# Four scan directions in a Mamba-like layer: two projections put into one product, and step sizes made chunk by chunk

## The chip, the cores and the metric

The kernel runs on one core of one Trainium2 chip, as one program. The metric is device time in microseconds, from three runs of the kernel before: 10589.44 us in the median, 10588.25 to 10604.14. A profile of one further execution shows where the time goes. The engines are named as in the profile: PE (TensorE, matrix products), PEld (its weight loads), DVE (VectorE), ACT (ScalarE), POOL (GpSimd) and SP (which here issues DMAs). Each engine takes its instructions in the order in which the program has them, and waits at an instruction until what it needs is there.

## What is computed

Four images of 96 channels and 64 x 64 pixels pass through six layers. The change lies in the first: a selective scan in four directions. Cut to what matters:

```python
xn = layernorm(x); xq, z = split(xn @ in_proj_w.T); z = silu(z)
xc = silu(depthwise_conv3x3(xq) + conv_b)          # 192 channels, L = 4096 pixels
x0 = xc by rows;  x1 = xc by columns
xs = [x0, x1, flip(x0), flip(x1)]                  # directions k = 0, 1, 2, 3
x_dbl = einsum('bkdl,kcd->bkcl', xs, x_proj_w)     # 6 + 16 + 16 rows per direction
dts, Bs, Cs = split(x_dbl, [6, 16, 16])
delta = softplus(einsum('bkrl,kdr->bkdl', dts, dt_w) + dt_b)   # the step sizes
h = exp(delta * A) * h + delta * u * B             # along the 4096 positions
y = sum over the 16 states of h * C, plus D * u
out = (layernorm(y0 + y1 + y2 + y3) * z) @ out_proj_w.T
```

Behind it come a deformable 3 x 3 convolution (offsets from a convolution, then gathers of pixels), a Fourier block of 192 channels, a feed-forward block, a linear attention and another feed-forward block.

## The kernel before

**Streams.** One loop (`Layer0.scan`) sets the order of everything. It goes through 1536 units: image, direction in the order 1, 3, 0, 2, four stretches of 1024 positions (backwards for directions 2 and 3), three groups of 64 channels, eight units of 8 channels x 16 states. Each unit is a load of `da` from HBM on ACT's queue (five buffers, four units ahead), an exponential on ACT (L725), a product on PE that spreads `du` (L730), on DVE a product with B (L741) and the scan (L744), on POOL a product with C (L755) and, for two units at a time, products on PE that sum the states (L772).

Between units the loop lets two other streams go on, each a chain of Python generators. `ends` prepares layer 0 for images 0, 1, 2, 3 one after another (`before`), then does the last layers of image after image, each as soon as that image is sampled. `middle` does layer 0's output part (`behind`, once the scans of the image have come far enough) and layer 1, the deformable convolution. A step of a stream is taken when the stream has credit (2.6 and 1.9 steps a unit) and while every engine has room by the costs that the steps name. A unit can be fetched only when its inputs are `ready`: while they aren't, the loop takes steps of `ends` alone, and no scan enters the order.

**The part that the change touches.** `before(b)` makes u for one image (`inputs`: normalisation and convolution; `us` holds 128 channels by rows, the same by columns, and the other 64 channels twice, by rows in the lower and by columns in the upper 64 partitions). Then it goes through 8 chunks of 512 positions twice: forwards for the pair of directions 0 and 1 (`pr` 0), backwards for 2 and 3 (`pr` 1). Directions k and k + 2 use the same u in the same order, since flipping is done by the scan, so a direction k + 2 differs from k only in its weights.

- `projected` makes, for each of the two directions of a pair, a product of 39 rows (32 of B and C, 6 of dts, one that stays 0) from two matmuls (L568 and L569, 128 and 64 channels), and ACT evicts it with a bias that makes the last row 1 (L570), into `xd0` or `xd1`, of which there is one buffer each. The 32 rows go to HBM (`bcd`).
- `steps` makes a step chain for 128 rows: t = 0 is the first direction's 128 channels, t = 1 the second's, t = 2 the other 64 channels of both. A matmul with 7 rows (L592), then on ACT abs, exp, log and two additions (L596 to L601), on DVE `rl` from `pd` and `lw` (L604), on POOL a difference (L605), on DVE another (L607: the step size, stored as `de`), on POOL the product with u (L610 or L616), and a split into three bf16 parts `du` over ACT, POOL, ACT and DVE (L622 to L628), stored on SP.
- `pipe` runs these chains four at a time, one started every three rounds. A round is one step of the stream. The order of chains in an image is one projection and three step chains, sixteen times.
- A unit of pair `pr` is ready when the two chunks under it are done up to t = 2.

After the last scan what is left is the end of image 3's output part, its layer 1, the rest of image 2's last layers and all of image 3's.

Of the kernel before, what the change touches and what calls it, by code (L numbers as in the profile page):

```python
# [8 lines left out]
F32 = mybir.dt.float32  # L9
# [24 lines left out]
NX = 2 * NS + R + 1  # L34
# [8 lines left out]
def prepare(x, **w):  # L43
# [25 lines left out]

    vecs[NX - 1, V_X1] = 1.0  # L70

# [6 lines left out]
    xp = np.concatenate([xp[:, R:], xp[:, :R], np.zeros((KG, 1, DI), f)], axis=1).transpose(0, 2, 1)  # L78
    a["xp_a"] = c(xp[:, :128].transpose(1, 0, 2))
    a["xp_c"] = c(np.stack([np.concatenate([xp[2 * p, 128:], xp[2 * p + 1, 128:]]) for p in range(2)], axis=1))  # L80
# [78 lines left out]
def cost(pe=0.0, dve=0.0, act=0.0, pool=0.0):  # L159
    return pe, dve, act, pool  # L160
# [212 lines left out]
class Layer0:  # L373
# [45 lines left out]
    def before(self, b):  # L419
        net = self.net  # L420
        tc, nc, ins = net.tc, net.nc, net.ins
        with tc.tile_pool(name=f"l0u{b}", bufs=1) as up:
# [3 lines left out]
            with tc.tile_pool(name=f"l0b{b}", bufs=1) as sm:  # L426
                xp_a, xp_c = (net.load(q, sm) for q in ("xp_a", "xp_c"))
                dtw = sm.tile([NX, KG, DI], F32, name=f"dtw{b}", tag="dtw", bufs=1)
                nc.sync.dma_start(dtw[2 * NS :], ins["dtw"])
                yield from pause(2)  # L430
                order = [(0, j) for j in range(NCH)] + [(1, j) for j in reversed(range(NCH))]
                xdbl = {}

                def chains():
                    yield self.projected(b, *order[0], us, xp_a, xp_c, sm, xdbl)
                    for n, (pr, j) in enumerate(order):
                        for t in range(3):
                            yield self.steps(b, pr, j, t, us, dtw, sm, xdbl)
                        if n + 1 < len(order):
                            yield self.projected(b, *order[n + 1], us, xp_a, xp_c, sm, xdbl)  # L440
# [115 lines left out]
    def projected(self, b, pr, j, us, xp_a, xp_c, sm, xdbl):  # L556
# [5 lines left out]
        for q in range(2):  # L562
            k = 2 * pr + q
            xd = sm.tile([NX, CH], F32, name=f"xd{b}_{k}_{j}", tag=f"xd{q}")
            hp = slice(64 * q, 64 * q + 64)
            ua = us[0][:, cs] if q == 0 else us[1][:, j * NR : (j + 1) * NR, :]
            px = net.mm(f"px{b}_{k}_{j}", NX)
            nc.tensor.matmul(px, lhsT=xp_a[:, k, :], rhs=ua, start=True, stop=False)  # L568
            nc.tensor.matmul(px, lhsT=xp_c[hp, pr, :], rhs=us[2][hp, cs], start=False, stop=True)  # L569
            nc.scalar.activation(xd, px, AF.Identity, bias=net.vec(V_X1, NX))  # L570
            xdbl[pr, j, q] = xd
            yield cost(pe=1.7, act=0.7)
        for q in range(2):
            nc.sync.dma_start(self.bc_d[b][2 * pr + q][:, cs], xdbl[pr, j, q][: 2 * NS])
        yield NOTHING

    def steps(self, b, pr, j, t, us, dtw, sm, xdbl):
# [55 lines left out]
        if t == 2:  # L633
            self.ready.add((b, pr, j))
# [895 lines left out]
```

## Time and profile before

| | us |
|---|---|
| median of three runs | 10589.44 |
| the profiled execution | 10462.69 |
| its span, first to last instruction | 10460.6 |
| DVE busy | 7640.0 (73%) |
| PE busy | 7119.7 (68%) |
| POOL busy | 6456.3 (62%) |
| ACT busy | 4352.7 (42%) |
| scans L744, 1152 + 384 | 2703.5 + 878.0 |
| projection products L568, L569, 256 records each | 234.5 + 186.3 busy |
| step products L592, 512 records | 324.5 busy |
| first scan starts at | 322.87 |
| last scan starts at | 8996 |
| last layers of image 3 alone, from about | 9790 |

A matmul with fp32 operands has two records in the trace. Busy time is the union of an engine's records, and PE's records overlap. In the profile a stretch of time is called by microseconds from the span's start. An instruction's idle time is the time in which its engine had nothing to do just before it, with the engine or DMA that ended this wait.

### The profile page before, as it was taken

The numbers are of one execution on the slowest core, as the hardware profiler recorded it, in microseconds if no ns is written. First come the engines' busy times: TensorE is split into PE (matmuls) and PEld (weight loads), VectorE is DVE, ScalarE is ACT, GpSimd is POOL, SyncE is SP. The second block draws the span as 40 slices with busy tenths as digits, with TensorE's granted clock in tenths as the row PEclk, the third lists the DMA queues.
The fourth block names the chain that finished last, engine by engine and source line by source line (L and its number), as shares of the span: only waits on it lengthen the run. The fifth ranks groups of instructions, "written<-read, shape, count | busy, mean of one in ns | idle before, by whom it ended". The sixth has DMA issues, their size and how long they took to land. (4 is left out here: it accounts for less than half of the span.)

```text
span 10460.6 us, 85850 instructions
## 1 busy us (share of the span) xinstructions
PE 7119.7 (68%) x28728; PEld 2481.0 (24%) x28728; DVE 7640.0 (73%) x4993; ACT 4352.7 (42%) x6950; POOL 6456.3 (62%) x3603
## 2 busy tenths in 40 slices
PE   7565865976794555558876665678676646877686
PEld 2010200311120111113332221133322112453262
DVE  0788688587759999987878889788888897444211
ACT  4564655665454443223433433333343423313223
POOL 0675476377537888875557878655678885366301
PEclk9555855866696666667777766677677666886695
DMA  1666565566656677776677667776767676543110
GB/s 45 166 174 157 149 173 162 140 172 168 156 134 171 184 188 185 189 181 161 177 184 184 169 160 190 172 179 166 186 174 176 174 188 151 118 137 92 52 45 6
DMA packets 775576, 1605.19 MB, mean 153 GB/s; under 512 B 249305, under 2 KB 339477, under 8 KB 773022
## 3 DMA queue, kind: packets, MB, share of 16 engines
q10 hardware_dynamic: 300672, 985.79, 37.4%
q1 hardware_dynamic: 400734, 387.34, 13.8%
q0 software_dynamic: 73728, 226.57, 8.3%
q8 instruction: 228, 3.74, 0.2%
q14 instruction: 214, 1.75, 0.1%
HBM read 1343.08 MB, written 256.29 MB: 153 GB/s over the span
## 5 line engine op out<-in xcount | busy, mean ns | idle before, releaser
L755 POOL TENSOR_TENSOR hc<-hh,bc 128x1024 f32<-128x1024 f32 x1536 | 3885.8, 2531 | 1937.3 <-DVE hh L744 1003.6
L725 ACT ACTIVATE da<-da,w_al 128x1024 f32<-128x1024 f32 x1536 | 1762.6, 1149 | 3126.4 <-DMA da<-de 981.5
L730 PE MATMUL db<-du,rep 96*128 96x512 bf16 x3072 | 1293.0, 515 | 2324.6 <-DVE hh L744 2147.1
L744 DVE TENSOR_TENSOR_SCAN hh<-da,st,db 128x1024 f32<-128x1024 f32 x1152 | 2703.5, 2347 | 165.4 <-ACT st L751 28.3
L741 DVE TENSOR_TENSOR db<-db,bc 128x1024 f32<-128x1024 f32 x1536 | 1871.0, 1218 | 585.3 <-PE db L730 585.0
L1074 POOL DMA_INDIRECT g<-table,idx x1152 | 1449.7, 1258 | 417.2 <-issue 191.1
L772 PE MATMUL py<-hc,w_fold 128*32 128x512 f32 x6144 | 1303.4, 886 | 25.4 <-POOL hc L755 8.8
L730 PEld LDWEIGHTS <-rep 96*128 96x128 bf16 x3072 | 231.2, 108 | 3539.8 <-DVE hh L744 2935.0
L744 DVE TENSOR_TENSOR_SCAN hh<-da,db 128x1024 f32<-128x1024 f32 x384 | 878.0, 2286 | 104.9 <-ACT st L751 31.5
L1085 DVE TENSOR_TENSOR g<-g,wt 128x3456 f32<-128x3456 f32 x128 | 593.1, 4634 | 148.6 <-DMA g<-table,idx 147.3
L605 POOL TENSOR_TENSOR w<-w,ex 128x512 f32<-128x512 f32 x192 | 259.0, 1349 | 650.7 <-ACT w L601 648.9
L518 PE MATMUL pc<-pad,wc 96*128 96x512 f32 x1152 | 533.1, 615 | 9.1 <-DMA wc<-wc_d 6.1
L607 DVE TENSOR_TENSOR rl<-rl,w 128x512 f32<-128x512 f32 x192 | 304.9, 1588 | 95.6 <-POOL w L605 95.3
L1102 PE MATMUL ps<-w_ident,s 128*96 128x128 f32 x1152 | 265.3, 378 | 136.9 <-DVE s L1091 120.7
L1332 POOL CAST xqf<-fl 96x512 fp8e5<-96x512 f32 x64 | 51.5, 810 | 496.6 <-DVE fl L1291 496.5
L604 DVE SCALAR_TENSOR_TENSOR rl<-pd,lw 128x512 f32<-128x512 f32 x192 | 130.7, 681 | 309.6 <-ACT lw L599 309.5
L592 PE MATMUL pd<-xd,dtw 7*128 7x512 f32 (+1 forms) x512 | 324.5, 953 | 43.9 <-ACT xd L570 28.5
L1103 ACT COPY st<-ps 96x384 f32<-96x384 f32 x384 | 177.5, 474 | 419.7 <-PE ps L1102 418.2
L772 PEld LDWEIGHTS py<-hc,w_fold 128*32 128x32 f32 x6144 | 184.8, 134 | 666.0 <-issue 516.2
L1109 PE MATMUL pd<-st,wdc 96*96 96x256 f32 x1152 | 309.0, 414 | 0.0
L518 PEld LDWEIGHTS pc<-pad,wc 96*128 96x128 f32 x1152 | 220.5, 195 | 310.5 <-issue 290.4
L628 DVE TENSOR_TENSOR du<-ex,du 128x512 bf16<-128x512 f32 x192 | 234.6, 1222 | 79.7 <-ACT du L626 75.3
(241 smaller groups left out, 10039.6 us busy)
## 6 DMA issues: line engine op xcount, KB each, us to landing
da<-de ACTq DMA_DIRECT2D x1536, 512.0 KB
du<-du ACTq DMA_DIRECT2D x384, 192.0 KB
bc<-bcd ACTq DMA_DIRECT2D x128, 512.0 KB
du<-du SPq DMA_DIRECT2D x128, 384.0 KB
y<-yb SPq DMA_DIRECT2D x384, 128.0 KB
de<-rl SPq DMA_DIRECT2D x128, 256.0 KB
m<-in_dft SPq DMA_DIRECT2D x128, 256.0 KB
du<-du SPq DMA_DIRECT2D x128, 192.0 KB
```

Source lines behind the costliest of these rows:

```text
L518: nc.tensor.matmul(pp, lhsT=wc[:, q, g * 128 : (g + 1) * 128], rhs=pad[:, r0 + dy : r0 + dy + NR, dx : dx + W], start=(q == 0), stop=(q == 8),
L592: nc.tensor.matmul(o, lhsT=dtw[2 * NS :, 2 * pr + q, m], rhs=xdbl[pr, j, q][2 * NS :], start=True, stop=True)
L607: nc.vector.tensor_sub(rl, rl, w1)
L725: self.net.nc.scalar.activation(u.da, u.da, AF.Exp, scale=self.al[:, a : a + 1])
L730: self.net.nc.tensor.matmul(db[:, h, :], lhsT=self.rep[:96, u.s % 4, :], rhs=u.du[u.s // 4][:, h * CH : (h + 1) * CH], start=True, stop=True,)
L741: nc.vector.tensor_mul(u.db, u.db, u.bc[:, 0, :])
L744: nc.vector.tensor_tensor_scan(u.along(u.hh), u.along(u.da), u.along(u.db), first, ALU.mult, ALU.add)
L755: self.net.nc.gpsimd.tensor_mul(u.hc, u.hh, u.bc[:, 1, :])
L772: nc.tensor.matmul(py[p0 : p0 + 32], lhsT=self.fold[:, u.i, :], rhs=hc[:, h * CH : (h + 1) * CH], start=u.add is None and u.i == 0, stop=( ...
L1074: nc.gpsimd.indirect_dma_start(out=g[:, k, :], out_offset=None, in_=self.tables[b % 2], in_offset=bass.IndirectOffsetOnAxis(ap=idx[:, 9 * ...
L1085: nc.vector.tensor_mul(g4, g4, w4.unsqueeze(2).to_broadcast([128, 36, C]))
L1109: nc.tensor.matmul(po, lhsT=wdc[:, k, :], rhs=st[:, k, :], start=(k == 0), stop=(k == 8))
```

## The change

The rows of directions k and k + 2 are made by one product: 32 rows of B and C and 6 of dts of direction q, the constant row at 38, zeros up to row 64, then 6 of dts of direction q + 2, a constant row at 70, and its 32 of B and C, 103 in all. The step weights of the second of the two are put at partitions 64 to 70, so that weights and rows stand in the same partitions. The loop over chunks is gone through once, forwards. A chunk has one call of `projected`, of two products (columns first), and six step chains: direction 1, the 64 other channels of 0 and 1, direction 3, the 64 of 2 and 3, direction 0, direction 2. Readiness is kept for each direction and each half of the channels (128 and 64), and a unit needs both halves of its two chunks. The cost named for a projection step goes from 1.7 to 1.9 on PE.

```diff
-NX = 2 * NS + R + 1
+NX = 64 + R + 1 + 2 * NS
...
-    vecs[NX - 1, V_X1] = 1.0
+    vecs[2 * NS + R, V_X1] = 1.0
+    vecs[64 + R, V_X1] = 1.0
...
+    xpp = np.zeros((2, NX, DI), f)
+    xpp[:, : 2 * NS] = xp[:2, R:]
+    xpp[:, 2 * NS : 2 * NS + R] = xp[:2, :R]
+    xpp[:, 64 : 64 + R] = xp[2:, :R]
+    xpp[:, 64 + R + 1 :] = xp[2:, R:]
...
-                dtw = sm.tile([NX, KG, DI], F32, name=f"dtw{b}", tag="dtw", bufs=1)
-                nc.sync.dma_start(dtw[2 * NS :], ins["dtw"])
+                dtw = sm.tile([64 + R + 1, 2, DI], F32, name=f"dtw{b}", tag="dtw", bufs=1)
+                for q in range(2):
+                    p0 = (2 * NS, 64)[q]
+                    nc.sync.dma_start(dtw[p0 : p0 + R + 1], ins["dtw"][:, 2 * q : 2 * q + 2])
...
-                order = [(0, j) for j in range(NCH)] + [(1, j) for j in reversed(range(NCH))]
...
-                    yield self.projected(b, *order[0], us, xp_a, xp_c, sm, xdbl)
-                    for n, (pr, j) in enumerate(order):
-                        for t in range(3):
-                            yield self.steps(b, pr, j, t, us, dtw, sm, xdbl)
-                        if n + 1 < len(order):
-                            yield self.projected(b, *order[n + 1], us, xp_a, xp_c, sm, xdbl)
+                    yield self.projected(b, 0, us, xp_a, xp_c, sm, xdbl)
+                    for j in range(NCH):
+                        for ks in ((1,), (0, 1), (3,), (2, 3), (0,), (2,)):
+                            yield self.steps(b, ks, j, us, dtw, sm, xdbl)
+                        if j + 1 < NCH:
+                            yield self.projected(b, j + 1, us, xp_a, xp_c, sm, xdbl)
...
-        for q in range(2):
-            k = 2 * pr + q
-            xd = sm.tile([NX, CH], F32, name=f"xd{b}_{k}_{j}", tag=f"xd{q}")
+        for q in (1, 0):
+            xd = sm.tile([NX, CH], F32, name=f"xd{b}_{q}_{j}", tag=f"xd{q}")
...
-            nc.tensor.matmul(px, lhsT=xp_a[:, k, :], rhs=ua, start=True, stop=False)
-            nc.tensor.matmul(px, lhsT=xp_c[hp, pr, :], rhs=us[2][hp, cs], start=False, stop=True)
+            nc.tensor.matmul(px, lhsT=xp_a[:, q, :], rhs=ua, start=True, stop=False)
+            nc.tensor.matmul(px, lhsT=xp_c[hp], rhs=us[2][hp, cs], start=False, stop=True)
...
-            yield cost(pe=1.7, act=0.7)
-        for q in range(2):
-            nc.sync.dma_start(self.bc_d[b][2 * pr + q][:, cs], xdbl[pr, j, q][: 2 * NS])
+            yield cost(pe=1.9, act=0.7)
+        for q in (1, 0):
+            nc.sync.dma_start(self.bc_d[b][q][:, cs], xdbl[q, j][: 2 * NS])
+            nc.sync.dma_start(self.bc_d[b][q + 2][:, cs], xdbl[q, j][64 + R + 1 :])
...
-            nc.tensor.matmul(
-                o, lhsT=dtw[2 * NS :, 2 * pr + q, m], rhs=xdbl[pr, j, q][2 * NS :], start=True, stop=True
-            )
+        for k in ks:
+            h, q = divmod(k, 2)
+            o, m = (pd[64 * q : 64 * q + 64], slice(128, DI)) if both else (pd, slice(0, 128))
+            rows = slice(64, 64 + R + 1) if h else slice(2 * NS, 2 * NS + R + 1)
+            nc.tensor.matmul(o, lhsT=dtw[rows, q, m], rhs=xdbl[q, j][rows], start=True, stop=True)
...
-        if t == 2:
-            self.ready.add((b, pr, j))
+        self.ready.update((b, k, both, j) for k in ks)
...
-                while not all((u.b, u.k // 2, 2 * u.j + h) in self.ready for h in range(2)):
+                while not all(
+                    (u.b, u.k, both, 2 * u.j + h) in self.ready for both in (False, True) for h in range(2)
+                ):
```

## The prediction

> **What bounds the kernel now.** I read four views in this order: the page (which engine is full, and when), the windows by stage, the waits of each stage, the timeline at the start. From the page:
>
> ```profile
> span 10460.6 us, 85850 instructions
> ...
> DVE  0788688587759999987878889788888897444211
> POOL 0675476377537888875557878655678885366301
> ...
> L604 DVE SCALAR_TENSOR_TENSOR rl<-pd,lw 128x512 f32<-128x512 f32 x192 | 130.7, 681 | 309.6 <-ACT lw L599 309.5
> L744 DVE TENSOR_TENSOR_SCAN hh<-da,st,db 128x1024 f32<-128x1024 f32 x1152 | 2703.5, 2347 | 165.4 <-ACT st L751 28.3
> ```
>
> VectorE carries the run of 1536 scans (one product at 1.22 us and one scan at 2.3 us each, about 3.55 us a unit) and is the fullest engine in most slices from the second to the 35th. Before it lies a start of 323 us, behind it a tail from 8996 us on. I cut the run at the scans between which a stage of the other work stands (columns: stretch, its length, busy us and counts of PE, weight loads, DVE, ACT, POOL, then clock, DMA share, GB/s):
>
> ```profile
> 323.00:422.00 99.00, 53.12 (x144) 7.58 (x144) 84.14 (x59) 54.14 (x88) 72.28 (x38) 0.60 0.64 173
> 1223.00:1761.00 538.00, 346.77 (x826) 52.88 (x830) 437.19 (x307) 328.61 (x523) 385.08 (x226) 0.59 0.64 171
> 1761.00:2063.00 302.00, 255.40 (x738) 82.45 (x730) 192.14 (x128) 167.54 (x197) 117.81 (x55) 0.84 0.53 141
> 2785.00:3093.00 308.00, 277.17 (x781) 88.46 (x780) 173.55 (x113) 166.16 (x220) 113.60 (x55) 0.89 0.53 135
> 3546.00:4074.00 528.00, 300.08 (x922) 67.39 (x919) 505.05 (x292) 246.60 (x397) 421.57 (x252) 0.62 0.69 184
> ```
>
> Row 1 is the first 20 units of image 0. Row 2 is the stage that the change rewrites, for image 1: 81 units in 538 us, 6.64 us each, DVE 81% busy. Row 3 is the convolution of image 2, PE at 85%, DVE waiting. Row 4 is the convolution of image 3 with the offset convolution of layer 1 on top, PE at 90%. Row 5 is image 3's steps beside sampling, DVE at 96%. So time here is DVE's work plus DVE's idle time, and only edits of that idle time count. The waits of row 2 and row 4 say what it is (us in total, times, longest):
>
> ```profile
> DVE rl L604 <- ACT lw L599: 35.3, 13, 15.8
> DVE rl L607 <- POOL w L605: 31.4, 26, 2.0
> DVE du L628 <- ACT du L626: 27.4, 10, 16.6
> ...
> PE db L730 <- DVE hh L744: 167.2, 55, 10.2
> ...
> ACT ex L596 <- PE pd L592: 27.6, 14, 4.7
> ...
> DVE db L741 <- PE db L730: 119.6, 29, 15.8
> ```
>
> In row 2 the scan's own input is early (PE waits 167 us for DVE); DVE loses its time inside the step chains, to ScalarE, which itself waits for the projections' and step products on PE. The last line is row 4: there PE is the bound.
>
> **What the Trainium skill says.** "Perfetto Trace Analysis", section Optimization Strategy: take the most contended engine, look at its gaps, and where regimes differ interleave them. The trace agrees that there are regimes (DVE 96% in row 5, 56% in row 4). "TensorE: Matmul & The Clock Gate", section LDWEIGHTS: a weight load is priced by its columns, not its rows; by it, 103 columns for 39 would add an estimated 53 ns a load. In the trace a load of 39 columns takes 141 ns (median, L568), more than the page's price, the loads of 128 and 64 columns at L592 a median of 184; both stand beside running matmuls, so I charge nothing. "GPSIMD Engine Reference", section Specifications: GpSimd shares VectorE's SBUF interface when DVE has two SBUF inputs. The trace agrees: L607 takes 0.69 us with POOL idle, 1.62 us beside it, 1588 ns on average. So packing chains denser doesn't cost DVE only its bare time; I use 3.5 us a chain (679 + 1588 + 1222 ns).
>
> **The change, part by part.**
>
> 1. Projections. Two directions in one product: 128 products fall away on PE (two records each, 0.95 us by the means 1012 and 817 ns, so 1.8 us: 235 us of PE) and 64 evictions on ACT (0.68 us: 44 us). A product over 512 columns costs the same with 103 output rows as with 39, by L592, whose 128 rows take a median of 1056 ns against 1047 for L568. Neither engine bounds these stages, so only the DVE waits behind them count. I sorted the idle time before the 192 instructions at L604 by their place among the three of a chunk: of 30, 35, 55 and 19 us for the images (the 170 us before the very first one left out) about 14, 27, 26 and 14 stand at the first, directly behind the projections; of L628's waits 8, 25, 12 and 7 at the third, whose bf16 casts share ACT with the evictions. That is some 130 us at 64 boundaries. Half the boundaries go: I take -55 us, from -20 (the chain merely waits for POOL instead) to -80.
>
> 2. Order by chunks, start. In the built program 10 chains instead of 7 stand ahead of the first scan, 22 instead of 13 ahead of scan 20, 34 instead of 19 ahead of scan 44: a unit needs both halves of its direction for two chunks, and a chunk now makes four directions first. Between the groups the scan stops in the program's order. Alone, chains run like this:
>
> ```profile
> 282.22 0.69 DVE L604 SCALAR_TENSOR_TENSOR rl<-pd,lw 128x512 f32<-128x512 f32 x1 [1.22 <-ACT lw L599]
> 285.54 0.68 DVE L604 SCALAR_TENSOR_TENSOR rl<-pd,lw 128x512 f32<-128x512 f32 x1
> 292.21 0.68 DVE L604 SCALAR_TENSOR_TENSOR rl<-pd,lw 128x512 f32<-128x512 f32 x1
> 302.34 0.69 DVE L604 SCALAR_TENSOR_TENSOR rl<-pd,lw 128x512 f32<-128x512 f32 x1 [1.22 <-ACT lw L599]
> ```
>
> Three chains in 20.1 us, 6.7 each, of which DVE works 3.5. Some 13 chains more run that way (3 ahead of the first scan, about 10 in two new pauses): 13 x 6.7 = 87 us of scan-free time, of which 13 x 3.5 = 46 us is DVE work that would have stood between scans anyway. Net +41 us, less up to 10 that units in flight cover, plus about 5 us for each restart, when ACT's queue holds the next loads behind the last step's store (at the first start a load kept ACT 18 us): +40 us. Bounds: -5, if flying units fill the pauses; +87, if the lighter units later don't run faster.
>
> 3. Order, later images. The rounds of a preparation fall from 192 to 168 (three per chain or projection: 64 against 56), so the stream gets on. Image 3's chains end at scan 512, not 603; its convolution starts about scan 345, beside layer 0's output part, and no longer beside the offset convolution (row 4, 120 us of DVE waiting for PE; row 3, the convolution without it, 79). Its chains then lie beside the offset convolution, where PE has the removed 60 us to spare. Against that, fewer chains lie in the full row 5. I count -25 us, from -60 to +30: no row shows this mixture, so rows 3 and 4 bound it.
>
> 4. Tail. Behind the last scan stand 32 fewer of the Fourier products (8 groups at about 1.1 us) and two more output products with their gating: -5 us, from -20 to 0.
>
> Nothing for the rest: as many stores of B and C rows (128), as many step stores on SP, one more weight load per image, all beside scans; if SP ran late it would show at ACT's loads, priced in 2. The unit of work per scan is unchanged.
>
> Sum: -55 + 40 - 25 - 5 = -45 us on the profiled execution's 10460.6, 0.43%. That execution took 10462.7 us in all, 1.2% below the 10589.4 median of the shown runs; I carry the ratio over: 10589.4 x 0.9957 = 10544.
>
> **Rivals.**
> Slower: the start decides. For: the pauses are in the order, and units 96 to 111, with hardly any chain beside them, still took 5.5 us. Against: units 0 to 44 ran at 4.7 with one chain to three. Price: +87, relief only -20, no gain by mixing: +67 us, 10657. It decides once lightened units stay above 5.2 us.
> No change: ACT and PE relief are swallowed, because chains come denser (image 1's 48 from scan 140 to 211 instead of 164 to 240) and L607 waits for POOL more; -20 + 40 - 15 - 5 = 0, 10590. For: POOL is at 72% in row 2 and its w-waits are already 31 us.
> Much faster: the pauses are filled and the mixture pays in full: -70 + 0 - 60 - 15 = -145, 10443. Against: the two pauses are six chains long, and only about two units fly.
> That the edit doesn't remove the products can't be: 128 instead of 256 stand on PE.
>
> **How the numbers follow.** Forecast 0.50 (its own range 10480 to 10590), slower 0.25, no change 0.17, much faster 0.08. The range 10450 to 10665 reaches the slower case and nearly the much faster one. A difference under 0.2% (21 us) can't be told from none here: faster 0.57, same 0.17, slower 0.26.
>
> **What would show it.** Projections: 128 records each at the two product lines, and DVE's waits of image 1's stage down from 94 us to about 70. Start: first scan near 338 us, DVE gaps near units 20 and 44, image 0's last chain near 790 us (831 now), its scan 96 no later than 880. Mixture: DVE waiting for PE during image 3's convolution under 120 us. I am wrong if scan 160 comes over 40 us late without being regained by scan 700, or if the time per unit in the stages of steps doesn't fall below 6.6 us.

## The result, and the profile after

The changed kernel takes 10632.65 us in the median of four runs (10618.27 to 10648.25), beside four runs of the kernel before at 10588.85 us (10575.49 to 10604.14). The ratio is 1.0041, with a 95% interval from 1.0021 to 1.0062: slower by about 44 us, where 45 us less had been forecast. Run again, on a chip where the kernel before takes about 10490 us, the changed kernel had the ratio 1.0053 (1.0034 to 1.0071). The record names no chip for the first runs. The profile of before, 10462.69 us, lies in the range of the later runs of that kernel (10458.58 to 10523.74) and not in that of its own (10575.49 to 10604.14), so it may belong to another chip than they do.

The page of the profile after; of the groups, those that answer to the lines shown of before:

```profile
span 10616.5 us, 85396 instructions
...
DVE  0787777687678999978888898787898977134211
...
POOL 0674665576467888845568888555688875156201
...
L755 DVE TENSOR_TENSOR_SCAN hh<-da,st,db 128x1024 f32<-128x1024 f32 x1152 | 2703.7, 2347 | 262.4 <-ACT st L762 91.0
...
L755 DVE TENSOR_TENSOR_SCAN hh<-da,db 128x1024 f32<-128x1024 f32 x384 | 878.1, 2287 | 53.0 <-ACT da L736 8.2
...
L614 DVE SCALAR_TENSOR_TENSOR rl<-pd,lw 128x512 f32<-128x512 f32 x192 | 131.3, 684 | 293.2 <-ACT lw L609 280.3
```

And of before, the scans that start without a state:

```profile
L744 DVE TENSOR_TENSOR_SCAN hh<-da,db 128x1024 f32<-128x1024 f32 x384 | 878.0, 2286 | 104.9 <-ACT st L751 31.5
```

Lines have moved: L604 of before is L614, L607 is L617, L628 is L638, L744 is L755. The digits of VectorE's first slices are lower (the second to the eleventh were 7886885877, now 7877776876), its idle time before the 1152 scans with a state has grown from 165 to 262 us, while before the 384 others it fell from 105 to 53 us: over all scans 315 us, where it was 270. The idle time before the first VectorE instruction of a chain has hardly moved, from 310 to 293 us, of which 170 us stand before the very first chain in both. The granted clock of PE is lower in this profile (0.689 on average, 0.702 before), but VectorE's idle time before the product with B, which PE ends, is nearly the same (592 us at L752, 585 at L741 before), so a slower PE shows little there.

The span of this profile is 156 us longer than that of before, more than the medians differ. Of these, 125 us lie behind the last scan (1589 us after it, 1464 before), and in the changed kernel's second profile that tail is 1501 us. So the two spans can't be subtracted. The tail of this profile is not used below, and only its part up to the last scan is read beside others.

Busy time of the changed kernel by stage (columns as in the prediction: stretch, length, busy us and counts of PE, weight loads, DVE, ACT, POOL, then clock, DMA share, GB/s). The first three rows are units 0 to 20, 20 to 44 and 44 to 96, the fourth is units 140 to 214 with image 1's step chains, the last units 399 to 462:

```profile
338.00:470.00 132.00, 69.47 (x161) 11.85 (x161) 108.67 (x77) 80.10 (x131) 93.44 (x56) 0.54 0.58 160
470.00:617.00 147.00, 84.01 (x192) 14.31 (x192) 115.58 (x84) 85.09 (x140) 102.78 (x61) 0.51 0.60 167
617.00:897.00 280.00, 139.24 (x369) 22.64 (x369) 245.78 (x187) 131.76 (x205) 186.10 (x107) 0.53 0.65 174
...
1168.00:1671.00 503.00, 279.78 (x694) 50.11 (x694) 402.58 (x292) 304.15 (x478) 365.70 (x218) 0.56 0.64 172
...
2868.00:3292.00 424.00, 285.76 (x713) 56.88 (x712) 339.93 (x251) 231.55 (x386) 281.71 (x169) 0.63 0.63 169
```

Before, units 0 to 20, 20 to 44 and 44 to 96 took 99, 109 and 320 us; the last two of these in the same view of the kernel before:

```profile
422.00:531.00 109.00, 67.55 (x175) 9.42 (x176) 98.88 (x66) 57.94 (x97) 79.91 (x42) 0.56 0.65 173
531.00:851.00 320.00, 211.65 (x462) 30.57 (x460) 271.80 (x193) 200.45 (x311) 241.54 (x142) 0.55 0.65 178
```

The two first stretches became 33 and 38 us longer and the third 40 us shorter: image 0's chains are moved ahead, and not all of the time they cost there comes back. What stands at the end of the first stretch is seen in the timeline of VectorE (start, duration; here the first instruction of each chain, then the scan's product):

```profile
430.96 0.69 DVE L614 SCALAR_TENSOR_TENSOR rl<-pd,lw 128x512 f32<-128x512 f32 x1
437.34 0.69 DVE L614 SCALAR_TENSOR_TENSOR rl<-pd,lw 128x512 f32<-128x512 f32 x1 [0.15 <-ACT lw L609]
447.48 0.69 DVE L614 SCALAR_TENSOR_TENSOR rl<-pd,lw 128x512 f32<-128x512 f32 x1 [1.22 <-ACT lw L609]
450.81 0.68 DVE L614 SCALAR_TENSOR_TENSOR rl<-pd,lw 128x512 f32<-128x512 f32 x1
457.44 0.69 DVE L614 SCALAR_TENSOR_TENSOR rl<-pd,lw 128x512 f32<-128x512 f32 x1 [0.15 <-ACT lw L609]
463.84 0.68 DVE L614 SCALAR_TENSOR_TENSOR rl<-pd,lw 128x512 f32<-128x512 f32 x1
...
468.08 1.22 DVE L752 TENSOR_TENSOR db<-db,bc 128x1024 f32<-128x1024 f32 x1
```

Six chains start in 33 us, 6.6 us apart on average, and no scan stands among them. This is the pause that the order contains.

The waits of VectorE while image 1's chains run (us in total, times, longest), in the changed kernel from 1155 to 1671 us:

```profile
DVE du L638 <- ACT du L636: 46.4, 16, 7.5
...
DVE rl L614 <- ACT lw L609: 35.8, 16, 14.4
...
DVE rl L617 <- POOL w L615: 17.7, 18, 2.0
```

Together 99.9 us, where the three lines of before had 94.1, and not the 70 of the prediction. The relief is not there.

### The profile page after: what moved, and what is told of

It reads as the page before. It is cut to its first block, busy times and chain, and to the rows that moved or that the text cites. A ratio compares the mean times of both kernels' runs of the same rounds, so it can differ in the third digit from the quotient of the medians.

```text
span 10616.5 us, 85396 instructions
## 1 busy us (share of the span) xinstructions
PE 7016.8 (66%) x28472; PEld 2521.1 (24%) x28472; DVE 7616.5 (72%) x4993; ACT 4313.2 (41%) x6886; POOL 6428.8 (61%) x3603
## 5 line engine op out<-in xcount | busy, mean ns | idle before, releaser
L741 PE MATMUL db<-du,rep 96*128 96x512 bf16 x3072 | 1296.8, 517 | 2494.0 <-DVE hh L755 2314.7
L755 DVE TENSOR_TENSOR_SCAN hh<-da,st,db 128x1024 f32<-128x1024 f32 x1152 | 2703.7, 2347 | 262.4 <-ACT st L762 91.0
L752 DVE TENSOR_TENSOR db<-db,bc 128x1024 f32<-128x1024 f32 x1536 | 1871.8, 1219 | 592.5 <-PE db L741 590.9
L783 PE MATMUL py<-hc,w_fold 128*32 128x512 f32 x6144 | 1274.0, 888 | 39.4 <-POOL hc L766 22.5
L741 PEld LDWEIGHTS <-rep 96*128 96x128 bf16 x3072 | 224.6, 107 | 3733.7 <-DVE hh L755 3095.0
L755 DVE TENSOR_TENSOR_SCAN hh<-da,db 128x1024 f32<-128x1024 f32 x384 | 878.1, 2287 | 53.0 <-ACT da L736 8.2
L604 PE MATMUL pd<-xd,dtw 7*64 7x512 f32 (+1 forms) x512 | 348.3, 1004 | 18.9 <-ACT xd L578 12.6
L1120 PE MATMUL pd<-st,wdc 96*96 96x256 f32 x1152 | 346.5, 451 | 3.2 <-issue 2.9
L638 DVE TENSOR_TENSOR du<-ex,du 128x512 bf16<-128x512 f32 x192 | 270.6, 1409 | 100.3 <-ACT du L636 92.7
L614 DVE SCALAR_TENSOR_TENSOR rl<-pd,lw 128x512 f32<-128x512 f32 x192 | 131.3, 684 | 293.2 <-ACT lw L609 280.3
L617 DVE TENSOR_TENSOR rl<-rl,w 128x512 f32<-128x512 f32 x192 | 238.7, 1243 | 105.9 <-POOL w L615 105.6
L986 PE MATMUL po<-pad,w_wom 96*27 96x512 f32 x576 | 293.3, 653 | 20.0 <-DVE rl L614 15.4
```

Of the source, the lines that this page charges most:

```text
L604: nc.tensor.matmul(o, lhsT=dtw[rows, q, m], rhs=xdbl[q, j][rows], start=True, stop=True)
L741: self.net.nc.tensor.matmul(db[:, h, :], lhsT=self.rep[:96, u.s % 4, :], rhs=u.du[u.s // 4][:, h * CH : (h + 1) * CH], start=True, stop=True,)
L752: nc.vector.tensor_mul(u.db, u.db, u.bc[:, 0, :])
L755: nc.vector.tensor_tensor_scan(u.along(u.hh), u.along(u.da), u.along(u.db), first, ALU.mult, ALU.add)
L783: nc.tensor.matmul(py[p0 : p0 + 32], lhsT=self.fold[:, u.i, :], rhs=hc[:, h * CH : (h + 1) * CH], start=u.add is None and u.i == 0, stop=( ...
L986: nc.tensor.matmul(po, lhsT=wom[:, k, :], rhs=pad[:, r0 + dy : r0 + dy + NR, dx : dx + W], start=(k == 0), stop=(k == 8),)
```

## The experiments

They ran on three chips, on each of which the kernel before takes 10487 to 10492 us in the median; each ratio is against runs of the kernel before on the same chip. The table gives from each profile when a scan starts, the time from the start of the last scan to the end of the span ("tail"), and the ratio.

| kernel | scan 0 | 44 | 96 | 609 | 882 | last scan | tail | ratio (95%) |
|---|---|---|---|---|---|---|---|---|
| before, profile shown at the start | 323 | 531 | 851 | 4074 | 5469 | 8996 | 1464 | |
| before, again | 323 | 534 | 851 | 4069 | 5470 | 9012 | 1477 | 1.0002 (0.9992 to 1.0012) |
| changed, profile above | 338 | 617 | 897 | 4106 | 5489 | 9028 | 1589 | 1.0041 (first runs) |
| changed, again | 338 | 615 | 897 | 4106 | 5492 | 9033 | 1501 | 1.0053 (1.0034 to 1.0071) |
| changed order, products apart | 348 | 644 | 927 | 4248 | 5619 | 9145 | 1520 | 1.0185 (1.0164 to 1.0206) |
| before, second pass without products | 324 | 531 | 848 | 4065 | 5465 | 9015 | 1479 | 0.9989 (0.9980 to 0.9999) |
| old order, rows kept in HBM | 322 | 531 | 850 | 4092 | 5498 | 9030 | 1487 | 1.0034 (1.0022 to 1.0046) |
| image 0 by pairs, others by chunks | 326 | 535 | 855 | 4056 | 5436 | 8995 | 1509 | 1.0007 (0.9998 to 1.0016) |
| image 0 by chunks, others by pairs | 340 | 617 | 897 | 4142 | 5519 | 9061 | 1501 | 1.0102 (1.0083 to 1.0121) |
| image 0 direction 1 first | 310 | 520 | 851 | 4063 | 5461 | 8998 | 1467 | 0.9987 (0.9977 to 0.9996) |
| image 0 by pairs, tail's order mended | 325 | 537 | 858 | 4074 | 5452 | 8993 | 1474 | 0.9986 (0.9974 to 0.9998) |
| before, tail's order spoilt | 322 | 529 | 847 | 4080 | 5470 | 9001 | 1525 | 1.0037 (1.0024 to 1.0050) |
| changed, tail's order mended | 338 | 616 | 899 | 4115 | 5488 | 9012 | 1501 | 1.0020 (1.0009 to 1.0030) |
| image 0 direction 1 first, tail's order mended | 309 | 515 | 843 | 4040 | 5433 | 8973 | 1476 | 0.9971 (0.9963 to 0.9978) |

How far a single profile may be trusted can be read from programs that are alike up to the last scan: three of before's order start it at 8996, 9012 and 9001, three of the changed order at 9028, 9033 and 9012, the two with image 0 by pairs at 8995 and 8993, the two with direction 1 first at 8998 and 8973. Up to scan 96 such programs agree within 8 us, at scan 609 within 23, and at scan 882 and the last one within 28. Smaller differences between single profiles show nothing, and ratios, which rest on several runs, are better evidence.

### The kernel before again

> The kernel before, unchanged, profiled a second time. Its first profile spans 10460.6 us with 1464 us after the last scan's start, while its other runs took 10575 to 10604 us. Theory 'the first profile was a lucky execution': this one spans about 10575 to 10600 us, with the difference of 115 to 140 us nearly all after the last scan (tail 1570 to 1600 us, as in the changed kernel, 1589) and the last scan still near 8996 us. Rival 'the change made the tail longer': this profile again has a tail of 1450 to 1480 us, and the changed kernel's 1589 us is its own loss.

It is the row "before, again" above: the ratio is 1.0002. The kernel's profile on this chip is 29 us longer than the one shown first (span 10489.4 against 10460.6), of which 16 us come in the last third of the scans and 13 us in the tail; its starts of scans in the table agree within 5 us up to 882. The short tail is there again, as the rival said. But the 1589 us don't belong to the changed kernel either: its own second profile, on the same chip as this one, has 1501.

### The changed order with the products apart

```diff
+            for p0, p1 in ((0, 39), (64, NX)):
-            px = net.mm(f"px{b}_{q}_{j}", NX)
-            nc.tensor.matmul(px, lhsT=xp_a[:, q, :], rhs=ua, start=True, stop=False)
-            nc.tensor.matmul(px, lhsT=xp_c[hp], rhs=us[2][hp, cs], start=False, stop=True)
-            nc.scalar.activation(xd, px, AF.Identity, bias=net.vec(V_X1, NX))
+                px = net.mm(f"px{b}_{q}_{j}_{p0}")[p0:p1]
+                nc.tensor.matmul(px, lhsT=xp_a[:, q, p0:p1], rhs=ua, start=True, stop=False)
+                nc.tensor.matmul(px, lhsT=xp_c[hp, p0:p1], rhs=us[2][hp, cs], start=False, stop=True)
+                nc.scalar.activation(xd[p0:p1], px, AF.Identity, bias=net.vecs[p0:p1, V_X1 : V_X1 + 1])
```

> The changed kernel with its order of chunks and chains, but each direction's 39 rows by a product of their own again: 128 products on PE and 64 evictions on ACT come back, at the same places in the order. Theory 'the merged product saves nothing, since neither engine bounds these stages': equal to the changed kernel within 15 us (ratio to before 1.003 to 1.006). Rival 'the merged product does save its 20 to 80 us, and the order costs more than it': 20 to 80 us slower than the changed kernel (ratio 1.006 to 1.012).

The ratio is 1.0185 against the changed kernel's 1.0053, slower than both expectations allowed, and the last scan starts 112 to 133 us later than in the three profiles of the changed order. That is more than twice the 55 us which the prediction gave for the products. The waits of image 1's stage, in this kernel from 1176 to 1741 us:

```profile
DVE du L639 <- ACT du L637: 68.0, 15, 8.9
ACT xd L579 <- PE px L578: 62.9, 28, 4.0
...
DVE rl L615 <- ACT lw L610: 46.8, 17, 21.6
```

In the changed kernel (again, same stage) these three are 47.5, 24.1 and 36.7 us. The products of a chunk now come in a burst: two in each of two rounds, and ScalarE, which evicts them, waits for PE and makes VectorE late. The step that makes them keeps its named cost on PE of 1.9 though it holds twice the work, so some of the loss may come from the loop's room being counted wrongly; this was not separated. So doubling the products in the *changed* order costs a great deal. That alone doesn't say that halving them in the *old* order saved as much, and the next two kernels ask for that.

### The old order without the second pass's products

```diff
         for q in range(2):
+            if pr == 1:
+                xdbl[pr, j, q] = xdbl[0, NCH - 1, q]
+                yield cost(pe=1.7, act=0.7)
+                continue
             k = 2 * pr + q
```

> The kernel before, in its own order, with the products and the evictions of the second pass left out (128 of 256 products, 64 evictions) and nothing in their place: the chains of directions 2 and 3 take the rows that the last chunk of directions 0 and 1 left, so these two directions are computed from the wrong rows. The steps of the stream and their costs stay. This is the relief of the change alone, without its order and without reloads. Theory 'the step chains don't wait for the projections in that order': scan 609 starts within 15 us of 4070 (before 4069 to 4074), the waits of DVE in image 1's stage stay at 80 to 100 us for lw, w and du together, ratio 0.998 to 1.001. Theory of the prediction (half the waits behind the projections go, 55 us): scan 609 at 3990 to 4050, the waits of image 1's stage near 70 us, ratio 0.993 to 0.997.

The ratio is 0.9989, about 12 us (1 to 21 us by the interval). Scan 609 starts at 4065, 4 to 8 us earlier than in the two profiles of before, less than such profiles differ; the last scan starts no earlier. Image 1's stage (1226 to 1755 us):

```profile
DVE du L632 <- ACT du L630: 35.0, 12, 16.2
DVE rl L608 <- ACT lw L603: 31.4, 12, 14.6
DVE rl L611 <- POOL w L609: 28.3, 24, 2.0
```

The sum is 94.7 us, against 94.1 with all the products. Over all four images, the idle time of the second pass alone at the two places that the prediction counted (the first `rl` of a chunk's first chain, the last `du` of its third) is 45 and 42 us in the two profiles of before, and 50 us here, where that pass has no product to wait for. The first theory, that the chains don't wait for the products where these are spread out, holds; the prediction's, with a ratio of 0.993 to 0.997, doesn't.

Another reading would be that a slower PE took back a larger gain. PE's granted clock is indeed lower here (0.690 to 0.696 in 14 runs, 0.699 to 0.704 in the 19 of the kernel before), and its other records are busy 79 to 93 us longer than in the two profiles of before. But VectorE's idle time before the product with B, which PE ends, is 587 us here and was 585 and 583, so there is no sign that this held VectorE up.

### The old order with the rows kept in HBM

```diff
+            if hs == (1,):
+                xd = sm.tile([64 + R + 1, CH], F32, name=f"xr{b}_{q}_{j}", tag=f"xr{q}")
+                nc.sync.dma_start(xd[dts], self.dts_d[b][q][:, cs])
+                xdbl[q, j] = xd
+                yield cost(pe=1.9, act=0.7)
+                continue
...
+            nc.sync.dma_start(self.dts_d[b][q][:, cs], xdbl[q, j][dts])
```

Products of 103 rows are made in the first pass; the second pass of an image loads its seven step rows back.

> The merged product alone: every instruction stands as in before, but the products of 103 rows are made in the first pass only; the seven rows of step sizes of directions 2 and 3 go to HBM and come back on SP in the second pass, where no product and no eviction is left (128 products and 64 evictions fewer). Theory 'PE time of the products is on the path, as the 118 us of the unmerged variant say': scan 609 starts 30 to 100 us before 4070, ratio 0.990 to 0.997. Rival 'in the old, spread order they cost only what DVE waits behind them, about 12 us an image at most': scan 609 0 to 30 us earlier, ratio 0.997 to 1.000. Below that: the reloads are late.

1.0034, so slower than before; scan 609 at 4092 is some 20 us late, which a single profile doesn't show for certain. As a test of the products' price it isn't clean, since the loads come late. The waits from 1226 to 1768 us:

```profile
DVE rl L633 <- ACT lw L628: 38.8, 14, 15.5
DVE du L657 <- ACT du L655: 36.5, 11, 16.9
DVE rl L636 <- POOL w L634: 32.4, 26, 2.0
PEld pd L623 <- DMA xr<-dts: 25.5, 6, 8.1
```

The three waits of VectorE are 107.7 us in all, not lower than before's 94.1, and the weight loads of the step products wait 25.5 us for the reloaded rows. It shows that this way of keeping the order doesn't pay; on the price of the products it decides nothing.

### Image 0 by pairs, the others by chunks, and the reverse

```diff
+                def pairs():
+                    order = [(0, j) for j in range(NCH)] + [(1, j) for j in reversed(range(NCH))]
+                    yield self.projected(b, 0, us, xp_a, xp_c, sm, xdbl, (0,))
+                    for n, (h, j) in enumerate(order):
+                        for ks in ((2 * h,), (2 * h + 1,), (2 * h, 2 * h + 1)):
+                            yield self.steps(b, ks, j, us, dtw, sm, xdbl)
...
-                yield from pipe(chains(), 4, every=3)
+                yield from pipe(pairs() if b == 0 else chains(), 4, every=3)
```

The second kernel has `chains() if b == 0 else pairs()`. In the pair order products of 103 rows are made in both passes, as many as before.

> The changed kernel, but image 0 is made in the order of before (directions 0 and 1 forwards, then 2 and 3 backwards, the products of 103 rows made in both passes); images 1 to 3 by chunks. Theory 'the start decides': scan 44 starts near 531 us as in before (617 in the changed kernel) and the whole time falls by 40 to 60 us, to before's (ratio 0.998 to 1.001). Rival 'the start is regained, the loss comes from the later images or the tail': scan 44 is early again, but the whole time stays within 15 us of the changed kernel (ratio 1.003 to 1.006).

> The complement: image 0 by chunks as in the changed kernel, images 1 to 3 in the order of before with products of 103 rows in both passes. Theory 'the start decides': as slow as the changed kernel (ratio 1.003 to 1.006), scan 44 near 617 us. Rival 'the later images or the tail': back at before's time or faster (ratio 0.998 to 1.001).

With the two kernels that were there, this makes a square; in each field the ratio, the start of the last scan and the tail:

| | images 1 to 3 by pairs | images 1 to 3 by chunks |
|---|---|---|
| image 0 by pairs | 1 / 8996 to 9012 / 1464, 1477 | 1.0007 / 8995 / 1509 |
| image 0 by chunks | 1.0102 / 9061 / 1501 | 1.0053 / 9033 / 1501 |

The first kernel behaves as the theory said: scan 44 starts at 535 us, and the ratio is back at 1.0007. The second is slower than both of its expectations.

Down the right column, where the changed kernel stands, image 0 by chunks costs 0.46% or 48 us; 30 of them are there when the last scan starts, if the means of all profiles with these orders are taken (9024 and 8994). Down the left column it costs 1.0%, with the last scan 49 to 65 us later. Along the first row the later images by chunks, with their 96 fewer products, change the ratio by no more than its interval, along the second they gain 0.5%. So the two parts don't simply add up, and why image 0 by chunks costs more ahead of pairs is not shown. Every field but the first has a tail 24 to 45 us longer, whichever image was changed. As far as single profiles show, the start accounts for the loss up to the last scan, and something else lengthens the tail.

### The order of the tail

Between scans and behind them the loop takes steps of two streams, and the number of steps that an image's preparation needs shifts what of `ends` faces what of `middle`. Counted in program order, the kernel before has 415 steps of image 2's last layers facing 390 steps of image 3's output part and sampling at the end; the changed one 403 facing 394. To test this, 16 steps of one stream are taken first when the scans are over; before them nothing differs:

```diff
+        for _ in range(16):
+            streams[1].step()
```

`streams[1]` is `middle`; in the kernel before, `streams[0]`, which is `ends`, was put first instead, to bring about there what the change brought about.

> The kernel before, unchanged up to the last scan, then 16 steps of image 2's last layers before the two streams alternate, so that they meet as in the changed kernel (399 against 390). Nothing else is changed. Theory 'the meeting of the streams': tail 1500 to 1520 us instead of 1464 to 1477, ratio to before 1.002 to 1.005. Rival: tail unchanged, ratio 0.998 to 1.001.

> The variant with image 0 in pairs, and behind the last scan 16 steps of the stream of output part and sampling before the two streams alternate. That restores how far the two stand apart there: in before 415 steps of image 2's last layers face 390 of the other, in the changed kernel 403 face 394. Theory 'the tail grew because the two streams meet differently': tail back to 1460 to 1480 us instead of 1509, the whole 25 to 40 us faster than that variant. Rival 'PE's clock or chance': tail stays at 1495 us or more.

> The changed kernel, and behind the last scan 16 steps of output part and sampling before the two streams alternate. Theory 'the loss is the start (about 45 us) and the meeting of the streams in the tail (about 25 to 35), and they add up': tail 1465 to 1480 us instead of 1501, ratio to before 1.001 to 1.003. Rival 'one cause': the tail's 24 us come from the later start and stay, ratio 1.004 to 1.006.

Spoilt, the kernel before has 1.0037. Mended, the kernel with image 0 by pairs goes from 1.0007 to 0.9986, its tail from 1509 to 1474 us, and the changed kernel from 1.0053 to 1.0020. Three rows of the windows view show the place: from the last scan to the first gather of image 3's sampling, to image 2's end (the last addition of its last block), to the end of the span. Before, again:

```profile
9012.00:9218.00 206.00, 175.40 (x1115) 96.13 (x1116) 39.38 (x64) 48.10 (x90) 20.40 (x22) 0.91 0.35 84
9218.00:9855.00 637.00, 431.40 (x2068) 249.36 (x2068) 274.50 (x184) 186.26 (x363) 418.54 (x322) 0.69 0.36 105
9855.00:10489.40 634.40, 467.48 (x3028) 268.03 (x3028) 86.17 (x122) 179.20 (x334) 36.72 (x34) 0.70 0.09 28
```

The changed kernel, again:

```profile
9033.00:9276.00 243.00, 213.29 (x1322) 119.21 (x1321) 45.65 (x73) 49.69 (x90) 25.33 (x26) 0.80 0.26 61
9276.00:9911.00 635.00, 423.50 (x1780) 237.50 (x1780) 271.95 (x177) 181.07 (x356) 402.19 (x322) 0.67 0.36 105
9911.00:10534.00 623.00, 455.68 (x3028) 267.46 (x3028) 86.20 (x122) 179.78 (x335) 37.34 (x34) 0.72 0.09 28
```

The first row of before with its tail spoilt:

```profile
9001.00:9246.00 245.00, 213.06 (x1402) 124.42 (x1400) 43.70 (x70) 52.63 (x97) 20.71 (x23) 0.85 0.30 71
```

And of image 0 by pairs with its tail mended:

```profile
8993.00:9203.00 210.00, 170.52 (x1045) 85.75 (x1040) 41.24 (x67) 45.38 (x84) 25.46 (x26) 0.90 0.31 71
```

From the first gather on, the stretches are alike: 637 against 635, 634 against 623. The first stretch is 206 us before and 243 after, and PE has 1115 matmul records there before, 1322 after. PE is busy 85% and 88% of it. Its granted clock was lower there too (0.80 after, 0.91 before), but its busy time per record is nearly the same, 161 and 157 ns. By that the clock accounts for some 5 of the 37 us (an estimate: 4 ns at 1322 records). Image 2's last products stand ahead of the offsets that the first gather needs, in PE's one order, and 207 records more in all make the gathers start 37 us later. All fourteen profiles agree: where 224 records of image 2's next Fourier transform (L1185 of before) stand ahead of the first gather, as in both profiles of the changed kernel and in the spoilt one, this stretch takes 242 to 247 us; where none does, 204 to 226 us. The whole tail of the changed kernel has fewer records (6130, where before has 6211), and is longer all the same. The mended one has 1045 records there and gathers after 210 us.

For the changed kernel with its tail mended, the runs show a gain, 0.33%, and the one profile doesn't show it in the tail. The first gather comes after 226 us instead of 243, with 1036 records of PE ahead instead of 1322, but what follows was 17 us longer, and the tail is 1501 us in both, not the 1465 to 1480 expected. Its profile is 22 us shorter than that of the changed kernel only ahead of the last scan, where the two programs are alike.

### Direction 1 first

```diff
+                    kinds = (((1,), (0, 1)), ((3,), (2, 3), (0,), (2,)))
...
-                        for ks in ((2 * h,), (2 * h + 1,), (2 * h, 2 * h + 1)):
+                        for ks in kinds[h]:
```

Image 0's first pass makes only the two chains of a chunk that direction 1 needs, the backward pass the other four. The other images go by chunks.

> As the variant with image 0 in pairs, but its first pass makes only what direction 1 needs (two chains a chunk instead of three), the second, backward pass the other four. Theory 'time is lost where the scan waits for chains': first scan near 310 us instead of 326, scan 44 near 515 instead of 535, scan 96 at most 10 us later than 855, the whole 10 to 20 us faster than that variant. Rival 'only DVE's total counts': scan 96 near 855 and the whole within 8 us of it.

> The variant whose first image makes direction 1 alone in its first pass, with the 16 steps ahead in the tail. If the gains add up: 20 to 35 us under that variant, ratio 0.995 to 0.997. If its tail of 1467 us was already as short as it gets: ratio 0.998 to 1.000.

With two chains a chunk the first scan starts at 310 us and scan 44 at 520, 11 to 15 us earlier than before. By scan 96 this lead is gone (851 us in both), and the last scan starts at 8998, no earlier than with image 0 by pairs (8995). The ratio is 0.9987, 21 us under that variant's, but in the profiles the gain lies in the tail: 1467 us against 1509, with 1104 records of PE ahead of the first gather instead of 1328. So it doesn't show that the gain comes from a scan that waits less for chains.

With 16 steps of `middle` first in the tail as well the ratio is 0.9971 (0.9963 to 0.9978), 10461.95 us against 10490.49: the fastest kernel of the study, just outside the 0.995 to 0.997 that was expected if the gains add up. In the profile its lead over the variant without those steps lies ahead of the last scan (8973), where the two programs are alike; its tail of 1476 us is no shorter than 1467. So the profiles don't show where this gain comes from. Nor was the kernel before given 16 steps of `middle` first, so how much of the 0.29% the new order of image 0 earns stays open.

## Why the prediction was wrong

**The step that failed first: part 1, the projections, -55 us.** The working found "some 130 us at 64 boundaries. Half the boundaries go". With the products of the second pass left out and nothing else touched, the three waits of image 1's stage are 94.7 us instead of 94.1, and the waits at the two places of the second pass are 50 us where they were 45 and 42. The ratio gives 12 us less (1 to 21), so the term measures -12 us, not -55, and lies outside its bounds of -80 to -20 but for the edge of the interval. The waits at those places were added up rightly (133 us). What was wrong was to put all of them down to the products. These two single instructions of the kernel before, from its timeline, are in the sum:

```profile
1244.91 0.69 DVE L604 SCALAR_TENSOR_TENSOR rl<-pd,lw 128x512 f32<-128x512 f32 x1 [15.79 <-ACT lw L599]
...
1475.51 0.69 DVE L628 TENSOR_TENSOR du<-ex,du 128x512 bf16<-128x512 f32 x1 [16.56 <-ACT du L626]
```

The first is image 1's very first chain, which waits because its pipeline starts. The same wait is 14.1 us in image 2 and 2.7 us in image 3, and the changed kernel has 14.4, 14.1 and 2.5 us in these places. The second comes once. ScalarE's timeline just ahead of it:

```profile
1456.74 0.68 ACT L570 ACTIVATE xd<-px,w_vecs 39x512 f32<-39x512 f32 x1 [3.08 <-PE px L569]
1472.64 0.62 ACT L622 CAST du<-ex 128x512 bf16<-128x512 f32 x1 [15.21 <-DMA du<-du]
1473.16 0.68 ACT L570 ACTIVATE xd<-px,w_vecs 39x512 f32<-39x512 f32 x1
1474.86 0.62 ACT L626 CAST du<-ex 128x512 bf16<-128x512 f32 x1
```

Both evictions of the products (L570) stand there, and take 0.68 us each. The 15.21 us go to a cast that waits for the store of an earlier `du`.

Without the 32.5 us of starts (15.8, 14.1 and 2.7), the first places held 48 of their 80.7 us, at 60 boundaries: 0.8 us each. The second and third places, which stand behind no projection, held 59 us at 128 chains, 0.46 us each. By these two figures some 20 us at the first places were more than a chain waits anyway, and half the boundaries are worth some 10 us (an estimate). Nor did the waits as a whole fall: over all four images the idle time before the three VectorE instructions of a chain was 140, 96 and 80 us (the very first wait left out) and is 124, 106 and 100 us in the changed kernel. The sum grew from 316 to 330. "Perfetto Trace Analysis", section Optimization Strategy, of the Trainium skill speaks of consistent bubbles, the same gap repeating over a stretch, as a possible sign of too few buffers. The waits of this trace were not of that kind: the lines named a longest wait of 15.8 and 16.6 us among 13 and 10, so they were not one gap repeated, and dividing them by the boundaries was not allowed.

The products have a price, but in another order: in the changed one the two products of a chunk stand together ahead of six chains, and with four there the last scan came 112 us or more later. The merge makes up for a bunching that the chunk order brings. It earns little where the products were already spread.

**Part 2, the start, +40 us: right, mechanism and size.** First scan at 338 us as built, pauses ahead of scans 20 and 44 of 6.6 us a chain, scan 96 at 897 us, 46 us late (the prediction had named 880 as the latest). At scan 44 it is 86 us, the 87 us of scan-free time in the working; 40 of these came back by scan 96, where 46 were counted as given back. By the ratios the start costs 36 us (from 0.9986 to 1.0020, both with the tail mended) or 48 us (from 1.0007 to 1.0053, both without). The price stood in the prediction; the gains that were to outweigh it were not there.

**Part 3, the mixture, -25 us: the mechanism half right, the gain given back.** VectorE's waits for PE during image 3's convolution were 133 us from unit 399 to 462, and 6 us in the units from 341 to 399. In the changed kernel image 3's preparation starts at unit 341, its convolution lies between units 363 and 395, and the offset convolution follows from 434; units 341 to 399:

```profile
DVE db L752 <- PE db L741: 89.6, 24, 7.1
```

Units 399 to 462:

```profile
DVE db L752 <- PE db L741: 45.0, 13, 6.4
```

In both stretches together the wait is 135 us, where it was 139. The first of them is under 120 us, as the prediction had asked, but the wait was moved and not removed. With image 0 by pairs it does fall, to 68 and 79 us in the two profiles of this order. There, however, the three waits of the chains between the first scan and scan 609 are 342 and 345 us, where the two profiles of before have 294 and 286, and scan 609 starts between 17 us earlier and 5 us later than before. Most of what VectorE no longer waits for PE comes back as waits in its chains.

Parts 1 and 3 together were forecast at -80 us. The kernel with image 0 by pairs and the tail mended has nearly only these two in it, with the product merged for three images of four: 0.9986, which is -15 us (-27 to -2).

**Part 4, the tail, -5 us: wrong in sign.** The records were counted and found fewer, which is so (6130 against 6211). What decides is how many of them stand ahead of the first gather: 1322 against 1115, and the tail is 24 to 37 us longer. That the two streams meet differently is a side effect of the fewer steps of an image's preparation; no term of the prediction had it. In the kernel before with its tail spoilt (1402 records) such a shift alone is worth 1.0037, 39 us.

So the sum reads, by ratios of kernels that differ in one thing each: -15 us for the later images and the merged products (0.9986), +36 for the start (1.0020), +35 for the tail (1.0053), 56 us in all (36 to 74); in the first runs it was 44 us. By the intervals each step is uncertain by some 20 us (an estimate). Taken in the other order, start after tail, they are -15, +22 for the tail and +48 for the start. Without the longer tail the kernel would still be slower (1.0020), and without the late start it would be even with before (1.0007).

Of the rivals, "the start decides" named the side and half of the place. Its price (87 us for the start, 20 of relief, nothing from the mixture and the tail: 67 us) is near the measured 44 and 56 us in part by luck: the tail makes up for what the start costs less. Units 44 to 96 ran at 5.4 us each (280 us by 52), above the 5.2 us from which that rival was to decide. The prediction's own signs of being wrong also came true: scan 160 starts 84 us late (1296 against 1213) and scan 700 still 54 us late (4603 against 4549), and the units of image 1's steps take 6.8 us (503 us by 74), not less than 6.6.

The claim that 103 rows cost what 39 cost held nearly. The larger of the two product lines after:

```profile
L576 PEld LDWEIGHTS px<-xa,w_xp_a x128: 165/248/298, 250.3 to 3487.9; 128*103 128x103 f32 x128
L576 PE MATMUL px<-xa,w_xp_a x128: 590/1047/1182, 250.3 to 3488.3; 128*103 128x512 f32 x128
```

And before (durations are shortest, median and longest, in ns):

```profile
L568 PEld LDWEIGHTS px<-xa,w_xp_a x256: 111/141/175, 250.5 to 3997.5; 128*39 128x39 f32 x128
L568 PE MATMUL px<-xa,w_xp_a x256: 592/1047/1077, 250.5 to 3998.4; 128*39 128x512 f32 x128
```

The median of this matmul is 1047 ns in both, the mean 978 ns after and 1012 before. Of the smaller one (64 channels, L569 before, L577 after) the mean rose from 817 to 884 ns and the median from 628 to 1054. Both lines together take 3.36 us for a product of 103 rows and 3.29 for one of 39 (busy time by the number of products). They are busy 206 us less in all (420.8 before, 214.9 after; the prediction's 235 us adds up records that overlap), PE as a whole only 103 us less (7119.7 to 7016.8), since other products took longer. In the old order, hardly anything waited for this time.

## What to carry to other kernels

Before an idle total is divided by a count, look at its longest waits: a start or a late store that comes once doesn't get rarer when its neighbours do, and leaving the suspected work out in the old order measures its price directly. A change of order is paid where the pipeline is empty: work made earlier than the first consumer needs it delays the start (here by 86 us at scan 44, by 46 at scan 96), so it is worth trying to give the first image the order that feeds the first consumer, and to keep the batched order for the rest. Where two streams share an in-order engine, count what stands ahead of the next long stage's first input, not only how much there is in all. And a start that is early in one profile is not yet a faster kernel: look at where the lead is a few hundred microseconds later.

## What the runs showed of the hardware

A weight load of 103 columns took 248 ns in the median, 107 ns more than one of 39 (141 ns). "TensorE: Matmul & The Clock Gate", section LDWEIGHTS, of the Trainium skill prices a load by its columns, from which the prediction estimated 53 ns more; the trace agrees on the direction, and the measured step is twice that for these fp32 loads, 1.7 ns a column. What the longer load itself costs the kernel was not separated.

The same kernel took 10588.85 us in its first runs and 10487 to 10492 us on the three chips of the later ones, nearly 1%, about twice the effect of the change. With 128 of the 256 products left out of the kernel before and nothing else touched, PE as a whole was busy only 103 to 110 us less, though the products themselves held some 200. The other 28216 records were busy 6813 us, where they had 6721 and 6734, and the mean granted clock was 0.690 to 0.696 in all runs, where it was 0.699 to 0.704 beside them. That the clock is the reason is not shown.

Sixteen steps of one stream, put ahead of the other's in the tail with the same work in all, moved the total by 0.2 to 0.4%, about as much as the change itself.
